# A count of the tiles that hold rows, and branches on TensorE that write zeros for steps past the count

## The chip, the cores and the metric

The kernel runs on one core of a Trainium2 chip. The time is that of one launch on the device, in microseconds (us). TensorE, the matrix engine, is called PE; VectorE is DVE, ScalarE is ACT, GpSimd is POOL, and SyncE, which issues most DMAs here, is SP. Each engine runs its own list of instructions in order, and waits on semaphores for the others.

## The reference

Two decoder layers over x, 16 sequences of 128 rows with 256 features, in float32. The first layer has causal attention with 16 heads, a recurrence over time in the place of cross attention, and a mixture of experts. The second has attention with 16 heads of 16 features, cross attention to a context with 16 heads of 128 features over 4 heads of keys and values, and a feed-forward part with ternary weights. The change concerns the mixture of experts, with 2048 rows, 16 experts, four experts for a row:

```
probs = softmax(h @ router_w.T)
top_vals, top_idx = top_k(probs, 4)
top_vals = top_vals / max(top_vals.sum(-1), 1e-09)
comb = zeros((N, E)).at[arange(N)[:, None], top_idx].add(top_vals)
g = einsum('nh,ehi->eni', h, w_gate)
u = einsum('nh,ehi->eni', h, w_up)
y = einsum('eni,eih->enh', silu(g) * u, w_down)
routed = einsum('enh,ne->nh', y, comb)
shared = silu(h @ sh_gate) * (h @ sh_up) @ sh_down
return routed + sigmoid(h @ sh_gate_w) * shared
```

## The kernel before

The kernel does not compute every expert for every row. While the shared expert runs, GpSimd scatters each normed row, four times, into a DRAM buffer `hs` that has a stretch of 2048 rows for each of the 16 experts. The rows of an expert stand together at the start of its stretch. Each stretch is cut into tiles of 128 rows. There are 8192 routed rows, so at least 64 tiles hold rows and at most 64+15 = 79 do; which ones, is known only at run time.

`tile_map` (L759 to L799) therefore builds a map on the chip. For every candidate tile DVE decides whether it holds rows (`per`, then `key`, which is 16 for a tile without rows and less for one with), ranks the candidates so that tiles with rows come first, and PE turns ranks into two lists of 128 numbers in `pmap`: the expert of the tile, and the row of `hs` where it starts. DVE copies them into `tmapT` (L798).

Then the pipeline at L1292 to L1296 works through the first NTILES = 79 entries of the map, whatever they hold, in NTILES + LAG = 85 steps. A step s works on several tiles at once, each in another stage:

- `fetch` (L746) for tile s, on SP: load the tile's start row from `tmapT` into a register, and start the DMA `hx <- hs`. The tile buffer has four slots.
- `turn_in` (L932) for tile s-2: two PE transposes into `pht`, and an ACT copy to `hxT`.
- `inner` (L941) for tile s-3: every eight tiles, PE loads eight expert numbers from `tmapT` (L943); gate and up products into `pgu` (L952); silu on ACT (L957), product with the up half on DVE (`eact`, L959).
- `turn_act` (L962) for tile s-5: two PE transposes into `pat`, a DVE copy to `eactT` (L968).
- `outer` (L971) for tile s-6: the down products into `pey` (L975), a copy `ey` on whichever of ACT and DVE the scheduler chooses (L981), and an SP store `hs <- ey`.

The four PSUM tiles `pht`, `pgu`, `pat` and `pey` come from one pool of four buffers, so that a stage takes over the buffer of the same stage a step before, or one like it, and waits for the copy or activation that read it.

After its stages each step calls `beside(s)` (L1226), which puts other work between the steps. It gathers finished rows back by GpSimd (`back_rows`, L1209: indirect DMAs out of `hs`), adds them to x on DVE (`back_sums`, L1218), and spreads the second layer's attention over the steps from 36 on: its scores `sc` (L1128) with maxima `nm` (L1131), `scT` (L1146) with exponents on ACT (L1150), values `zsT` (L1158), `zq` (L1169) with the division `z` on DVE (L1174), and the transposes `pqT` and `pkT` (L1105) of what DVE prepares in `spread` (L1110). At step 81 it issues the loads of the cross attention's weights Wk, Wq and Wv on SP (L1256); Wo follows after the last step (L1264). Cross attention begins with `pk` (L1315) and `proj` (L1349).

The order of PE's instructions in this part is the order in which the code is written (`tc.manual_schedule(engines={ET})`); the order on the other engines is chosen by a scheduler, from estimated times, within what the data allow. The loop is unrolled when the program is built, and before the change the program has no branch but the one with which every engine enters it.

```
for s in range(NTILES + LAG):
    for f, lag in ((fetch, 0), (turn_in, 2), (inner, 3), (turn_act, 5), (outer, LAG)):
        if 0 <= s - lag < NTILES and not (f is fetch and s in where):
            f(s - lag)
    beside(s)
```

Of the kernel before, what the change touches and what calls it, by code (L numbers as in the profile page):

```python
# [17 lines left out]
P = 128  # L18
B = 16
S = 128  # L20
D = 256
NK = D // P
# [8 lines left out]
TOPK = 4  # L31
IMOE = 176
# [4 lines left out]
NTILES = B * TOPK + E - 1  # L37
# [15 lines left out]
def decoder(ctx, tc, a, out):  # L53
    nc = tc.nc
    V, A, PE, GP = nc.vector, nc.scalar, nc.tensor, nc.gpsimd
# [701 lines left out]
    tmapT = rt.tile([1, 2, P], I32, name="tmapT")  # L757

    def tile_map():  # L759
# [169 lines left out]
    psum2.close()  # L929
    pools["wide"] = ctx.enter_context(tc.tile_pool(name="wide", bufs=4, space=PSUM, side="right", reuse_waits="tile"))  # L930

    def turn_in(j):  # L932
        hx = live[j]
        pt = tps.tile([P, NK, P], F32, tag="t", name="pht")
        for k in range(NK):
            PE.transpose(pt[:, k, :], hx[:, k * P : (k + 1) * P], ident)  # L936
        hT = mp.tile([P, NK, P], F32, tag="hxT", name="hxT")
        A.copy(hT, pt)  # L938
        live[j] = hT

    def inner(j):  # L941
        if j % NB == 0:
            _, vals = nc.values_load_multi_w_load_instructions(  # L943
                tmapT[0:1, 0, j : j + NB], engines=[ET], min_val=0, max_val=E - 1,
                skip_runtime_bounds_check_because=why,
            )
            for i, v in enumerate(vals):
                held[j + i] = v
        hT = live[j]
        pg = tps.tile([P, 2 * IMOE], F32, tag="t", name="pgu")  # L950
        for k in range(NK):
            PE.matmul(  # L952
                pg, hT[:, k, :], wgu[:, k, bass.ds(held[j], 1), :].rearrange("p e i -> p (e i)"),
                start=k == 0, stop=k == NK - 1,
            )
        s = mp.tile([P, IMOE], F32, tag="esilu", name="esilu", bufs=2)
        A.activation(s, pg[:, :IMOE], AF.Silu)  # L957
        act = mp.tile([P, IMOE], F32, tag="eact", name="eact")
        softmax.last = V.tensor_tensor(act, s, pg[:, IMOE:], ALU.mult).ins  # L959
        live[j] = act  # L960

    def turn_act(j):  # L962
        act = live[j]
        pt = tps.tile([P, NK, P], F32, tag="t", name="pat")
        for k in range(2):
            PE.transpose(pt[:HM, k, :], act[:, k * HM : (k + 1) * HM], ident)  # L966
        aT = mp.tile([HM, 2, P], F32, tag="eactT", name="eactT")
        V.tensor_copy(aT, pt[:HM])  # L968
        live[j] = aT

    def outer(j):  # L971
        aT = live.pop(j)
        py = tps.tile([P, D], F32, tag="t", name="pey")
        for k in range(2):
            ins = PE.matmul(  # L975
                py, aT[:, k, :], wd[:, bass.ds(held[j], 1), k, :].rearrange("p e d -> p (e d)"),
                start=k == 0, stop=k == 1,
            )
        last_pe[:] = [ins.ins]
        y = mp.tile([P, D], F32, tag="ey", name="ey")  # L980
        nc.any.tensor_copy(y, py)  # L981

        ins = nc.sync.dma_start(hs[bass.ds(where[j], P), :], y).ins
        for group in ("stores", "fetches", "gathers"):
            tc.declare_no_dep(ins, group=group, reason="each tile has rows of its own")
        tc.add_to_no_dep_group("stores", ins)

# [230 lines left out]


    LAG, FIRST, APART = 6, 36, 2
    GATHER = TOPK + E - 1 + LAG + 2
    LEAD = 6 * NKV

# [399 lines left out]
```

## Time and profile before

| what | value |
|---|---|
| median of 3 runs | 1679.83 us (1673.32 to 1681.09) |
| the profiled execution | 1683.29 us |
| its span, first to last instruction | 1681.6 us |
| mean granted clock of TensorE | 0.986 of full |
| first full product of an expert's tile on PE (step 3) | 762.25 us |
| a full step, from `pht` to the next `pht` | 2.50 us (1008.90 to 1011.39) |
| last `pey` (step 84) | 1032.42 us |
| first `proj` of cross attention | 1033.31 us |
| DMA `hx <- hs`, issue to landing | 2.1 us |
| DMA `hs <- ey`, issue to landing | 1.9 us |
| the ten loads of expert numbers on PE's sequencer | 0.588 to 0.779 us each |

The profile is of one execution; its times are counted from the start of the span. A line of a timeline gives start and duration in us, the engine, the line of the code, the operation, output and inputs by the names of the program, the partitions and elements, and how many instructions are put together in it; a bracket at the end is the time that the engine had stood idle and the work that released it. "PEld" are PE's weight loads, which run beside its matmuls. In the lines of the table of windows stand the stretch, its length, the busy time of PE, PEld, DVE, ACT and POOL with their counts, PE's granted clock, the share of the DMA engines and GB/s. The section on queues has, for each, packets, megabytes and the share of the 16 DMA engines' time.

### The profile page before, as it was taken

To read this page: it belongs to the slowest core of one execution; us is meant where nothing else is said; L and a number is where in the kernel's file an instruction comes from. 1 tells how busy PE (TensorE), PEld (TensorE's weight loads), DVE (VectorE), ACT (ScalarE), POOL (GpSimd) and SP (SyncE) were. 2 spreads that over 40 slices of the span, in tenths; PEclk is the share of its full clock that TensorE was granted. 3 is DMA by queue.
4 is the path that set the end of the run, shared out by engine and by line. 5 is a ranking of instruction groups with operands and counts; after the bars stand their busy time and mean duration, and the time that the engine had idled before them with its cause. 6 is when DMAs were issued, how large, how long until landed. Compare 5 with 4: busy or idle time off the path is not lost.

```text
span 1681.6 us, 27336 instructions
## 1 busy us (share of the span) xinstructions
PE 1630.0 (97%) x9824; PEld 1152.2 (69%) x9824; DVE 957.4 (57%) x2491; ACT 808.2 (48%) x2205; POOL 569.2 (34%) x586
## 2 busy tenths in 40 slices
PE   8999999999999999999899999999999999999996
PEld 4666666666665685656576777777777777787774
DVE  2333486457536667623345556567666666666756
ACT  3444454445444444113334545666666666665553
POOL 2010132244024234031246445654444444432420
PEclk9999999999999999999999999999999999999998
DMA  9990000000000019123353335000000000000000
GB/s 301 404 352 1 0 7 7 20 26 20 0 26 32 7 40 270 42 80 113 99 154 107 107 96 176 17 11 14 8 8 7 8 8 8 8 8 10 4 4 13
DMA packets 91662, 110.24 MB, mean 66 GB/s; under 512 B 8647, under 2 KB 66951, under 8 KB 91527
## 3 DMA queue, kind: packets, MB, share of 16 engines
q1 hardware_dynamic: 83094, 89.55, 16.5%
q0 software_dynamic: 6144, 16.79, 3.2%
q10 hardware_dynamic: 2288, 2.14, 0.4%
q8 instruction: 79, 1.29, 0.3%
q14 instruction: 57, 0.46, 0.1%
HBM read 54.06 MB, written 54.39 MB: 64 GB/s over the span
## 4 chain that ended last, share of the span: by engine, by line
PE 53%; DVE 2%; ACT 2%; issue 1%; POOL 1%; DMA 1%; SPq 0%; POOLq 0%; ACTq 0%; DVEq 0%
PE acc_x L1415 6%; PE proj L1349 6%; PE pgu L952 5%; PE pey L975 4%; PE sc L1380 3%; PE z L1400 3%; PE acc_sh L732 2%; PE pg L714 2%; PE pu L714 2%; PE pkv L1089 2%; PE pk L1315 2%; PE pT L1392 2%; PE pv L1315 1%; PE ss L1363 1%; PE sc L1128 1%
## 5 line engine op out<-in xcount | busy, mean ns | idle before, releaser
L189 ACT ACTIVATE sc<-sc,nmax 128x128 f32<-128x128 f32 x512 | 198.9, 389 | 169.9 <-DVE nmax L186 140.4
L186 DVE TENSOR_REDUCE nmax<-sc 128x4 f32<-128x512 f32 x128 | 87.3, 682 | 162.8 <-POOL sc L589 160.9
L589 POOL TENSOR_SCALAR_AFFINE_SELECT sc<-sc 128x512 f32<-128x512 f32 x64 | 42.9, 670 | 318.6 <-ACT sc L588 313.4
L1349 PEld LDWEIGHTS proj<-hc,wbig 128*128 128x128 f32 x1024 | 124.0, 192 | 29.2 <-issue 23.7
L125 POOL TENSOR_TENSOR rq<-rq,mhalf 128x4 f32<-128x4 f32 x64 | 67.8, 1059 | 209.7 <-DVE rq L1372 193.5
L595 PE MATMUL projv<-wv,hT 128*128 128x512 f32 x256 | 124.2, 608 | 3.3 <-ACT qT L578 3.3
L1415 PE MATMUL acc_x<-wbig,zT 128*128 128x256 f32 x512 | 124.8, 386 | 0.7 <-ACT zT L1406 0.7
L1349 PE MATMUL proj<-hc,wbig 128*128 128x128 f32 x1024 | 124.6, 275 | 0.1
L576 PE MATMUL proj<-hT,wq 128*128 128x512 f32 x256 | 122.6, 602 | 0.5 <-ACT hT L156 0.5
L576 PE MATMUL proj<-hT,wk 128*128 128x512 f32 x256 | 120.9, 595 | 1.1 <-ACT sc L588 1.0
L174 PEld LDWEIGHTS acc_l<-wo,zT 128*128 128x128 f32 x512 | 96.4, 190 | 36.6 <-issue 26.6
L174 PE MATMUL acc_l<-wo,zT 128*128 128x256 f32 x512 | 121.3, 380 | 0.0
L952 PE MATMUL pgu<-wbig,hxT 128*128 x316 | 111.8, 478 | 2.1 <-PE pht L936 0.8
L1415 PEld LDWEIGHTS acc_x<-wbig,zT 128*128 128x128 f32 x512 | 93.3, 190 | 23.6 <-issue 11.3
L125 POOL TENSOR_TENSOR ss<-ss,mhalf 128x32 f32<-128x32 f32 x16 | 87.5, 5471 | 45.7 <-DVE ss L1098 45.6
L189 ACT ACTIVATION_READ_ACCUMULATOR sc<-sc,nmax 128x1 f32 x512 | 95.5, 187 | 0.0
L1383 DVE SCALAR_TENSOR_TENSOR sc<-sc,rq,mask 128x128 f32<-128x128 f32 x256 | 77.5, 343 | 29.0 <-PE sc L1380 24.0
L1209 POOL DMA_INDIRECT back<-hs,idx x64 | 64.1, 1002 | 84.4 <-DMA hs<-ey 68.0
L576 PEld LDWEIGHTS proj<-hT,wk 128*128 128x128 f32 x256 | 48.7, 191 | 64.1 <-issue 52.6
L968 DVE COPY eactT<-pat 88x256 f32<-88x256 f32 x79 | 33.0, 418 | 98.2 <-PE pat L966 98.2
L624 PEld LDWEIGHTS z<-probT,v 128*128 128x128 f32 x512 | 68.1, 194 | 30.2 <-issue 29.9
L975 PE MATMUL pey<-wd,eactT 88*128 x316 | 84.7, 391 | 0.9 <-ACT hxT L938 0.9
(344 smaller groups left out, 3508.3 us busy)
## 6 DMA issues: line engine op xcount, KB each, us to landing
hs<-zero SPq DMA_DIRECT2D x16, 2048.0 KB, 19.0
hx<-hs SPq DMA_DIRECT2D x79, 128.0 KB, 2.1
hs<-ey SPq DMA_DIRECT2D x79, 128.0 KB, 1.9
wbig<-in_L_ffn_w_gate_dram SPq DMA_DIRECT2D x2, 1408.0 KB, 13.6
wbig<-in_L_ffn_w_up_dram SPq DMA_DIRECT2D x2, 1408.0 KB, 17.1
wd<-in_L_ffn_w_down_dram SPq DMA_DIRECT2D x2, 1408.0 KB
wq<-in_L_attn_W_Q_dram SPq DMA_DIRECT2D x8, 256.0 KB, 4.0
vT<-in_ctxT_dram ACTq DMA_DIRECT2D x8, 256.0 KB, 2.5
```

Of the source, the lines that this page charges most:

```text
L125: power.last = GP.tensor_tensor(v, v, mhalf[:, :n], ALU.pow).ins
L174: ins = PE.matmul(acc[:, t, :], zT[:, i, :], w[:, h0 + i, :], start=False, stop=last and i == 3, skip_group_check=True,)
L186: softmax.last = V.tensor_reduce(nmax, sc, AX.X, ALU.max, negate=True).ins
L189: A.activation(p[:, i, :], sc[:, i, :], AF.Exp, bias=nmax[:, i : i + 1], accum_out=rs[:, i : i + 1])
L576: PE.matmul(pj, w[:, k, h, :], hTs[g][:, k, :], start=k == 0, stop=k == NK - 1)
L595: PE.matmul(pv, hTs[g][:, k, at], wv[:, k, 4 * hq : 4 * hq + 4, :].rearrange("p h e -> p (h e)"), start=k == 0, stop=k == NK - 1,)
L624: PE.matmul(pz[:, i, :], v[:, i, :], pT[:, i, :], start=True, stop=True)
L952: PE.matmul(pg, hT[:, k, :], wgu[:, k, bass.ds(held[j], 1), :].rearrange("p e i -> p (e i)"), start=k == 0, stop=k == NK - 1,)
L975: ins = PE.matmul(py, aT[:, k, :], wd[:, bass.ds(held[j], 1), k, :].rearrange("p e d -> p (e d)"), start=k == 0, stop=k == 1,)
L1349: PE.matmul(pj[:, i, :], wqx[:, n, k, i * DH : (i + 1) * DH], hTs[b][:, k, :], start=k == 0, stop=k == NK - 1,)
L1383: V.scalar_tensor_tensor(sc[:, i, :], psc[:, i, :], rq[:, i : i + 1], mask, ALU.mult, ALU.add)
L1415: PE.matmul(accs[b][:, :D], zT[:, i, :], wox[:, 4 * n + i, :], start=n == 0 and i == 0, stop=n == NKV - 1 and i == 3,)
```

## The change

The map also counts the tiles with rows: DVE compares each `key` with 15.5, two PE products with a column of ones sum the result into a free column of `pmap`, and DVE copies the sum into `nusedT`. The four stages no longer issue their work when called. Each returns three things: a function that issues its products on PE, the PSUM tile they write, and a function that issues the rest (copy, silu, product on DVE, store). A step first issues all its products, then all rests. The expert numbers are loaded ahead of the step's products (`numbers`).

From step SURE = 64+6 = 70 on the products stand in a branch on PE, with the count in a register that is loaded at step 70: if the count is above s-6, the number of the oldest tile in the step, the products are done; otherwise, when none of the step's tiles holds rows, PE writes zeros into the same PSUM tiles, with one matmul of a single row for each. The rests and `beside(s)` are done in either case.

```diff
+        used = rt.tile([P, 2], F32, name="used")
+        V.tensor_scalar(used, key, float(B) - 0.5, None, ALU.is_lt)
...
+            for h in range(2):
+                PE.matmul(
+                    pmap[0:1, 2 * P : 2 * P + 1], ones[:, 0:1], used[:, h : h + 1], start=h == 0, stop=h == 1,
+                )
+        V.tensor_copy(nusedT, pmap[0:1, 2 * P : 2 * P + 1])
         V.tensor_copy(tmapT, pmap[0:1, : 2 * P].rearrange("p (j n) -> p j n", j=2))
...
     def turn_in(j):
         hx = live[j]
         pt = tps.tile([P, NK, P], F32, tag="t", name="pht")
-        for k in range(NK):
-            PE.transpose(pt[:, k, :], hx[:, k * P : (k + 1) * P], ident)
-        hT = mp.tile([P, NK, P], F32, tag="hxT", name="hxT")
-        A.copy(hT, pt)
-        live[j] = hT
+
+        def products():
+            for k in range(NK):
+                PE.transpose(pt[:, k, :], hx[:, k * P : (k + 1) * P], ident)
+
+        def rest():
+            hT = mp.tile([P, NK, P], F32, tag="hxT", name="hxT")
+            A.copy(hT, pt)
+            live[j] = hT
+
+        return products, pt.rearrange("p k n -> p (k n)"), rest
...
     LAG, FIRST, APART = 6, 36, 2
+    SURE = B * TOPK + LAG
...
             for s in range(NTILES + LAG):
-                for f, lag in ((fetch, 0), (turn_in, 2), (inner, 3), (turn_act, 5), (outer, LAG)):
-                    if 0 <= s - lag < NTILES and not (f is fetch and s in where):
-                        f(s - lag)
+                if s < NTILES and s not in where:
+                    fetch(s)
+                if 0 <= s - 3 < NTILES:
+                    numbers(s - 3)
+                if s == SURE:
+                    nused = nc.values_load(
+                        nusedT[0:1, 0:1], engines=[ET], min_val=SURE - LAG, max_val=NTILES,
+                        skip_runtime_bounds_check_because=why,
+                    )
+                stages = [
+                    f(s - lag) for f, lag in ((turn_in, 2), (inner, 3), (turn_act, 5), (outer, LAG))
+                    if 0 <= s - lag < NTILES
+                ]
+
+                with tc.If(nused > s - LAG) if s >= SURE else ExitStack() as some:
+                    for products, _, _ in stages:
+                        products()
+                if s >= SURE:
+                    with some.Else():
+                        for _, t, _ in stages:
+                            PE.matmul(t, zeros_b[:, : t.shape[0]], zeros_b[:, : t.shape[1]], start=True, stop=True)
+                for _, _, rest in stages:
+                    rest()
                 beside(s)
             load_last_weights()
```

`inner`, `turn_act` and `outer` are split in the same way. `outer` no longer records its last product in `last_pe`.

In the built program the branch is laid out in line: at each of the 15 steps PE has a compare with a branch, the block of products with a jump over the block of zeros, and the block of zeros with a jump to what follows. Each of the other four engines has a jump at the same place of its list, although it has nothing in either block. Where the scheduler cut a list, instructions no longer change places across the jump: from step 70 on SP issues each fetch after the store of the step before, where it had two fetches and then two stores.

More of the change, by code (lines that the diff above doesn't have):

```diff
@@ L757, in decoder @@
     tmapT = rt.tile([1, 2, P], I32, name="tmapT")
+    nusedT = rt.tile([1, 1], I32, name="nusedT")
     def tile_map():
@@ L934, in turn_in, with numbers @@
         pt = tps.tile([P, NK, P], F32, tag="t", name="pht")
-        for k in range(NK):
-            PE.transpose(pt[:, k, :], hx[:, k * P : (k + 1) * P], ident)
-        hT = mp.tile([P, NK, P], F32, tag="hxT", name="hxT")
-        A.copy(hT, pt)
-        live[j] = hT
-    def inner(j):
+        def products():
[6 more added lines that the diff above has]
+        return products, pt.rearrange("p k n -> p (k n)"), rest
+    def numbers(j):
         if j % NB == 0:
@@ L948, in inner, with products, rest @@
                 held[j + i] = v
+    def inner(j):
         hT = live[j]
         pg = tps.tile([P, 2 * IMOE], F32, tag="t", name="pgu")
[L951 to L960, printed above, removed]
+        def products():
+            for k in range(NK):
+                PE.matmul(
+                    pg, hT[:, k, :], wgu[:, k, bass.ds(held[j], 1), :].rearrange("p e i -> p (e i)"),
+                    start=k == 0, stop=k == NK - 1,
+                )
+        def rest():
+            s = mp.tile([P, IMOE], F32, tag="esilu", name="esilu", bufs=2)
+            A.activation(s, pg[:, :IMOE], AF.Silu)
+            act = mp.tile([P, IMOE], F32, tag="eact", name="eact")
+            softmax.last = V.tensor_tensor(act, s, pg[:, IMOE:], ALU.mult).ins
+            live[j] = act
+        return products, pg, rest
     def turn_act(j):
@@ L964, in turn_act, with products, rest @@
         pt = tps.tile([P, NK, P], F32, tag="t", name="pat")
[L965 to L969, printed above, removed]
+        def products():
+            for k in range(2):
+                PE.transpose(pt[:HM, k, :], act[:, k * HM : (k + 1) * HM], ident)
+        def rest():
+            aT = mp.tile([HM, 2, P], F32, tag="eactT", name="eactT")
+            V.tensor_copy(aT, pt[:HM])
+            live[j] = aT
+        return products, pt[:HM].rearrange("p k n -> p (k n)"), rest
     def outer(j):
@@ L973, in outer, with products, rest @@
         py = tps.tile([P, D], F32, tag="t", name="pey")
[L974 to L986, printed above, removed]
+        def products():
+            for k in range(2):
+                ins = PE.matmul(
+                    py, aT[:, k, :], wd[:, bass.ds(held[j], 1), k, :].rearrange("p e d -> p (e d)"),
+                    start=k == 0, stop=k == 1,
+                )
+        def rest():
+            y = mp.tile([P, D], F32, tag="ey", name="ey")
+            nc.any.tensor_copy(y, py)
+            ins = nc.sync.dma_start(hs[bass.ds(where[j], P), :], y).ins
+            for group in ("stores", "fetches", "gathers"):
+                tc.declare_no_dep(ins, group=group, reason="each tile has rows of its own")
+            tc.add_to_no_dep_group("stores", ins)
+        return products, py, rest
     U = B * NKV
@@ L1292, in decoder @@
             for s in range(NTILES + LAG):
[L1293 to L1295 removed]
+                if s < NTILES and s not in where:
[6 more added lines that the diff above has]
+                        skip_runtime_bounds_check_because=why,
+                    )
+                stages = [
[11 more added lines that the diff above has]
+                    rest()
                 beside(s)
```

## The prediction

> **What bounds the kernel now.** I read the page's busy times first, then the timeline of TensorE (PE) around the steps the change touches, then all engines there, then the table of windows.
>
> ```profile
> PE 1630.0 (97%) x9824; PEld 1152.2 (69%) x9824; DVE 957.4 (57%) x2491; ACT 808.2 (48%) x2205; POOL 569.2 (34%) x586
> ...
> q8 instruction: 79, 1.29, 0.3%
> ```
>
> PE is busy 97% of the span, so PE work taken out pays in full wherever nothing else is late. The second line is used below. Whether something else is late is read where the work is taken out. PE in the last steps of the pipeline (start, duration, line, tile):
>
> ```profile
> 1015.08 0.44 PE L936 MATMUL pht<-ident,hx 128*128 128x128 f32 x2
> 1015.35 1.35 PE L952 MATMUL pgu<-wbig,hxT 128*128 x4
> 1016.54 0.38 PE L966 MATMUL pat<-ident,eact 128*88 128x128 f32 x2
> 1016.76 1.03 PE L975 MATMUL pey<-wd,eactT 88*128 x4
> 1017.62 0.38 PE L936 MATMUL pht<-ident,hx 128*128 128x128 f32 x2
> ...
> 1020.04 1.13 PE L975 MATMUL pey<-wd,eactT 88*128 x4 [0.22 <-ACT hxT L938]
> 1021.10 1.08 PE L1158 MATMUL zsT<-probT,vaug 128*32 128x128 f32 x32
> ...
> 1028.49 1.15 PE L1128 MATMUL sc<-kT,qT 16*128 16x128 f32 x26 [0.33 <-DVE z L1174]
> ...
> 1033.31 3.74 PE L1349 MATMUL proj<-hc,wbig 128*128 128x128 f32 x32
> ```
>
> The first four lines are step 79, 1015.08 to 1017.62. A bracket says how long PE stood idle and for whom: here PE already waits a little, for ACT at 1020.04 and for DVE at 1028.49. The other engines in the same stretch:
>
> ```profile
> 1015.76 2.07 ACT L1150 ACTIVATE probT<-scT 128x512 f32<-128x512 f32 x4
> ...
> 1017.69 0.40 ACT L938 COPY hxT<-pht 128x256 f32<-128x256 f32 x1
> ...
> 1018.11 1.28 ACT L957 ACT_TABLE_LOAD   x1
> ...
> 1019.41 0.32 ACT L957 ACTIVATE esilu<-pgu 128x176 f32<-128x176 f32 x1
> ...
> 1020.76 0.68 DVE L1110 TENSOR_TENSOR spread<-qk,ss 128x512 f32<-128x512 f32 x1
> ...
> 1028.02 0.42 DVE L1174 TENSOR_TENSOR z<-zq,rs 128x256 f32<-128x256 f32 x1
> ...
> 1029.48 2.48 DVE L1131 TENSOR_REDUCE nm<-sc 128x4 f32<-128x512 f32 x4 [1.04 <-PE sc L1128]
> ```
>
> To see: ACT is in four exponents, a copy, a table load and a silu from 1015.76 to 1019.73 without a gap, and DVE's spread, z and maxima (nm) sit between PE's pieces. These two chains end only 0.3 to 1 us before PE wants them.
>
> **The change part by part.**
>
> How many steps skip. The reference's router on these inputs gives 73 tiles with rows (the sum over experts of rows/128, rounded up; one expert is a row over a tile's edge, so 72 is possible). Step s branches on nused > s-6, so steps 70 to 78 do their products and 79 to 84 write zeros.
>
> PE work removed. A full step is 2.50 us apart in the timeline (1008.90 to 1011.39): pht 0.22, pgu 1.19, pat 0.22, pey 0.87, from start to next start. Steps 79 to 84 hold 2 pht, 3 pgu, 5 pat and 6 pey: 0.44+3.57+1.10+5.22 = 10.33 us. Zeros added: 16 one-row matmuls of bf16. Row L165 has the same form with 512 columns, two in 0.60 us where one takes 0.374, so 0.22 each; at 256 to 352 columns I take 0.12, in all 1.9 us. If PE set the pace everywhere, the gain would be 8.4 us.
>
> What of it reaches the end. Copies, silu, products on DVE, stores and gathers all stay, and a zero matmul waits for its PSUM tile just as the product did (four buffers, four stages a step). So I walk the stretch with PE short.
> - Step 79's zeros are done near 1015.7. Step 80's pey needs the tile that silu and eact of step 79 read. ACT reaches that silu at 1019.41 whatever PE does, since the exponents wait for scT, which is unchanged. Eact follows near 1020.1, so zsT starts near 1020.4 (before 1021.10): of 4.5 us saved 0.7 arrive.
> - pqT waits for spread, 0.68 on DVE behind eact: near 1021.75 (before 1022.11). Gain here 0.4.
> - Steps 81 and 82 write five zeros in place of 3.4 us of products: zq near 1023.7 (before 1026.40), 2.7 ahead.
> - sc's fourth tile needs DVE's z, which stands behind back_sums' adds (1.51 for two at 1026.07, another 0.43), and these behind gathers that wait for stores. I place z's end between 1025.8 and 1026.6 (before 1028.44): 1.9 to 2.6 ahead.
> - Then 2.48 of maxima on DVE, eactT, pey of steps 83 and 84, and proj. The first proj also needs Wq from DMA: issued 1024.28, landed 5.8 later, near 1030.1, now queued on SP behind a store. proj starts 1031.0 to 1031.75 against 1033.31.
>
> So 1.5 to 2.4 us arrive, taken as 2.0; the rest of the 8.4 becomes PE waiting for ACT, DVE and DMA.
>
> The count. One DVE compare and one 1x1 copy (about 0.15 each) before the map's copy, hidden because the first fetch needs the map long before PE reaches step 2 at 761.35, and two tiny fp32 matmuls (4 records; the pmap row L794 has its records 0.11 apart) inside a stage where PE is at 1.00: +0.3 us.
>
> Products ahead of rests. Up to step 69 PE's order is unchanged; one hxT copy stands behind a weight activation of 0.55 on ACT, but is wanted a step (2.5 us) later: 0. From 70 on each SP fetch comes behind the store of the step before: it lands 2.1 us after issue (page, hx), wanted 1.1 later: 0, and up to 1 us a step if that cover is gone. The numbers' load (0.6 us, L943) moves ahead of pht, under the sequencer's lead (1.6 us in steady steps): +0.1.
>
> The branches, which no row of before shows as such. PE gets a compare at each of 15 steps and one jump in a true step, two when false; ACT, DVE, POOL and SP get a jump a step, and what is queued behind theirs are the copies, silus, adds and stores above, for which PE waits. Lower bound 0: PE's sequencer runs 1.6 us ahead in full steps. Nearest row: all engines jump once at the start, between a barrier at 0.69 to 0.74 and first instructions at 0.80 to 0.90, so at most 0.17 each. In steps 70 to 78 it hides (no engine but PE is near full there): +0.1. In 79 to 84 some four jumps lie in the ACT, DVE and PE chain: +0.6. [...]
>
> The clock. [...] At 787.47 PE had been idle 2.42 us, and the clock fell for the next matmuls (last but third figure: PEclk):
>
> ```profile
> 785.00:790.00 5.00, 2.58 (x12) 1.88 (x12) 1.00 (x3) 2.71 (x8) 1.09 (x3) 0.90 0.38 79
> 790.00:795.00 5.00, 5.00 (x20) 3.52 (x19) 1.07 (x4) 1.28 (x4) 0.00 (x0) 0.76 0.67 243
> ```
>
> The step begun at 788.59 ended at 792.77, 4.18 in place of 2.50: one such drop costs 1.7 us. [...] By the row the waits of 1.5 to 2.5 us that my walk leaves near 1022 and 1025 can each bring another: 0 to 3.4, part of it under waits for other engines. I take 0.9, half a drop.
>
> Sum: -2.0 +0.3 +0.1 +0.1 +0.6 +0.9 = 0.0 us. The profiled execution took 1683.3 us (span 1681.6), and its like after would take 1683.3; the median of the three runs of before is 1679.8, and I forecast 1679.8. The runs of before spread over 7.8 us, so 0.5%, or 8.4 us, is about what a measurement of this kernel can tell from no change.
>
> **The rivals.**
>
> A. The skipped work lands whole: -8.4+0.3 = -8.1, 1671.7. For it: PE at 97%. Against it: the ACT chain to 1019.73 and the brackets above, which leave PE no room to move up. Chance 0.07.
>
> B. Slower: a jump throws away what the sequencer had fetched, and each is paid by a new fetch. Price: the page's q8 line has 79 packets in 0.3% of 16 engines over the span, 1.0 us each; with a DMA's way from issue to landing (2.1 for hx), some 2 us a jump. Place: steps 70 to 84 on PE, 9+12 jumps. The sequencer's lead is then gone at each step, so 1 to 2 us are bare in a true step (9 to 18 us) and 12 to 24 in the false ones, of which the skipped work pays up to 8: +13 to +34, taken as +20, 1700. It decides from 0.56 us bare a step (8.4/15). For it: fetches are sequential in the trace, one packet behind the other. Against it: the jump at the start at 0.17 or less. Chance 0.28 that over 8.4 us are lost, this or jumps of 0.6 to 1.2 each.
>
> C. The change doesn't do what it says: the count reads 79, or steps go true, and nothing is skipped. Then +0.5 for count and order, +0 to 2.4 for branches: near 1681. The count itself, 73 of 79, argues against it. Chance 0.04.
>
> **How the numbers follow.** About unchanged, by my walk, 0.61; A 0.07 (its -8.1 lies at the bound; with the runs' spread I put 0.05 beyond it); B 0.28; C 0.04, within 0.5%. So faster by over 0.5% 0.05, within 0.67, slower 0.28. The range goes from 1673, short of A, to 1700, B's value: 0.07 is left out below and 0.13 above.
>
> **What would show it.** TensorE from 1015 to 1033: 16 short zero matmuls in place of pht to pey; zsT near 1020.4, behind silu and eact of step 79; proj's first near 1031.4; PE idle there up by 6 us, named ACT and DVE; the clock in windows after 1017. Steps 70 to 78 still 2.50 us apart; if each is 3 us or more with idle put down to issue, B is right. proj at 1025 would be A; full pgu after 1017, C. I am wrong if the slow place lies before step 70, where I cost the new order at nothing.

## The result and the profile after

The changed kernel takes 1679.08 us, median of 20 runs (1676.15 to 1686.52); the kernel before takes 1675.15 (1671.52 to 1682.36) in as many, of which the three that the prediction had to go by lay high. The ratio is 1.0028, with an interval of 1.0018 to 1.0039: slower by some 4.7 us, within the 0.5% that the prediction set as the bound of no change, but with the sign certain. The forecast of 1679.8 us stood for no change against the median of three runs, and that median came down by 4.7 us with 20.

The two profiled executions do not show the loss at first sight: the span after is 1679.9 us against 1681.6. The table of windows tells why. The first two rows are of before, the next two of the changed kernel (stretch, its length, busy time of the five engines, PE's granted clock, DMA share, GB/s):

```profile
780.00:800.00 20.00, 17.13 (x73) 12.06 (x74) 4.45 (x16) 7.59 (x22) 4.56 (x8) 0.91 0.39 121
800.00:850.00 50.00, 44.18 (x185) 30.97 (x185) 15.23 (x45) 18.61 (x53) 13.56 (x21) 0.90 0.35 107
```

```profile
780.00:800.00 20.00, 17.84 (x85) 12.75 (x86) 4.87 (x16) 8.23 (x24) 4.55 (x8) 1.00 0.43 135
800.00:850.00 50.00, 44.40 (x209) 31.45 (x208) 19.10 (x55) 20.10 (x59) 16.93 (x25) 1.00 0.39 121
```

The execution of before that was profiled happened to lose clock here (0.91 and 0.90, against 1.00 in the changed kernel's), long before the change acts; it had 1683.3 us, 8 above its kernel's median. The work there is the same in both kernels. From pey of step 6 to pey of step 49 it took 133.6 us (768.18 to 901.81), the changed kernel's 126.4 (767.74 to 894.09). So spans can't be set against each other; stretches of the timeline can, from one event to another. I use three, in us:

- A, from pey of step 69 to the first scT of step 78: the steps that branch and do their products.
- B, from that scT to the first proj: the steps that skip.
- C, from that proj to the first pkT of cross attention: what follows.

| | A | B | C |
|---|---|---|---|
| before | 34.7 | 19.3 | 6.2 |
| changed, this profile | 38.6 | 20.5 | 6.1 |

The change loses 3.9 us in A, where it was to cost next to nothing, and 1.2 in B, where the walk was to gain 2 before the clock and the jumps. B in the changed kernel, on PE (start, duration, line, tile; in the bracket the idle time before it and what ended it):

```profile
1010.48 1.17 PE L1182 MATMUL scT<-q2T,kT 32*128 32x128 f32 x32
1011.47 0.27 PE L1350 MATMUL pht<-zeros_b 1*128 1x256 bf16 x1
1011.58 0.31 PE L1350 MATMUL pgu<-zeros_b 1*128 1x352 bf16 x1
...
1014.65 0.36 PE L1350 MATMUL pat<-zeros_b 1*88 1x256 bf16 x1 [1.04 <-ACT hxT L952]
1016.65 0.39 PE L1350 MATMUL pey<-zeros_b 1*128 1x256 bf16 x1 [1.64 <-DVE eact L982]
1016.97 1.93 PE L1194 MATMUL zsT<-probT,vaug 128*32 128x128 f32 x32
1018.83 1.12 PE L1141 MATMUL pqT<-ident,spread 128*128 128x128 f32 x4
...
1026.38 3.78 PE L1372 MATMUL pk<-wbig,hc 128*128 128x512 f32 x4 [0.37 <-DVE nm L1167]
...
1030.98 3.84 PE L1406 MATMUL proj<-hc,wbig 128*128 128x128 f32 x32 [0.51 <-ACT ey L1015]
```

To see: the zeros cost what they were taken for (0.11 from one to the next), PE waits for ACT and DVE as foreseen, and then zsT takes 1.93 in place of 1.08, pqT 1.12 in place of 0.66, pk 3.78 where the same four products take 1.88 later on. That is half speed. The windows of the same stretch say it in the clock (last but third figure):

```profile
1010.20:1013.60 3.40, 2.47 (x40) 1.57 (x39) 3.01 (x12) 2.99 (x5) 3.40 (x2) 1.00 0.12 41
...
1013.00:1016.00 3.00, 0.93 (x3) 0.26 (x3) 0.25 (x1) 2.97 (x6) 2.13 (x5) 0.60 0.13 44
1016.00:1019.00 3.00, 2.35 (x34) 1.65 (x35) 1.91 (x6) 1.11 (x5) 2.39 (x3) 0.50 0.29 87
...
1025.00:1028.00 3.00, 2.63 (x18) 1.54 (x15) 2.37 (x4) 0.37 (x1) 0.00 (x0) 0.50 0.96 323
```

In A two things are to be seen. On DVE, at step 75, the division z stands behind adds and copies, where in the profile of before it followed the reciprocal directly. The first two rows are of before, the others of the changed kernel:

```profile
997.60 0.26 DVE L1172 RECIPROCAL rs<-zq 128x16 f32<-128x16 f32 x1
997.89 0.42 DVE L1174 TENSOR_TENSOR z<-zq,rs 128x256 f32<-128x256 f32 x1
```

```profile
990.62 0.26 DVE L1208 RECIPROCAL rs<-zq 128x16 f32<-128x16 f32 x1 [1.97 <-PE zq L1205]
990.79 0.39 DVE L1254 SCALAR_TENSOR_TENSOR x<-back,wts,x 128x256 f32<-128x256 f32 x1
991.10 0.33 DVE L982 TENSOR_TENSOR eact<-esilu,pgu 128x176 f32<-128x176 f32 x1
991.35 0.48 DVE L1254 SCALAR_TENSOR_TENSOR x<-back,wts,x 128x256 f32<-128x256 f32 x1
991.75 0.41 DVE L997 COPY eactT<-pat 88x256 f32<-88x256 f32 x1
992.08 0.41 DVE L1210 TENSOR_TENSOR z<-zq,rs 128x256 f32<-128x256 f32 x1
```

PE's sc then waits 0.80 us for z, and the pgu that follows, at 994.51, takes 2.37 in place of 1.35: the clock again, at half for 3.41 us from 993.15, which is worth 1.7 us of full work. And on ACT, in seven of the nine steps from 70 to 78, hxT is released by the wrong product (in the other two ACT was busy until then):

```profile
1006.61 0.37 ACT L952 COPY hxT<-pht 128x256 f32<-128x256 f32 x1 [1.17 <-PE pat L993]
1006.88 0.32 ACT L980 ACTIVATE esilu<-pgu 128x176 f32<-128x176 f32 x1
1007.59 0.37 ACT L1015 COPY ey<-pey 128x256 f32<-128x256 f32 x1 [0.38 <-PE pey L1008]
```

pht began at 1004.90 and was done by 1005.3, but hxT, which copies it, starts at 1006.61, with pat. In the trace PE's semaphore is not raised between the end of pht and the end of pgu at 1006.47, and hxT starts with the raise of the first pat; in the profile of before it was raised at the end of pht. The built program gives the reason: both sides of this step's branch raise the semaphore by 8 in all, the side of the products by 4 at the end of pgu and by 1 with each product of pat and pey, and pht's products do not raise it by themselves. The pgu of the next step then waits up to 0.24 us for ey. No wait of PE in A is for a load of hx, so the order of fetches behind stores on SP cost nothing that shows.

### The profile page after: what moved, and what is told of

Its sections match the earlier page's. It is cut to its first block, busy times and chain, and to the rows that moved or that the text cites. A ratio compares the mean times of both kernels' runs of the same rounds, so it can differ in the third digit from the quotient of the medians.

```text
span 1679.9 us, 27293 instructions
## 1 busy us (share of the span) xinstructions
PE 1623.6 (97%) x9794; PEld 1146.7 (68%) x9794; DVE 956.9 (57%) x2493; ACT 806.9 (48%) x2205; POOL 568.2 (34%) x586
## 4 chain that ended last, share of the span: by engine, by line
PE 53%; DVE 3%; ACT 2%; issue 1%; POOL 1%; DMA 0%; POOLq 0%; SPq 0%; ACTq 0%; DVEq 0%
PE proj L1406 7%; PE acc_x L1472 6%; PE pgu L973 5%; PE sc L1437 3%; PE pey L1008 3%; PE z L1457 3%; PE acc_sh L732 2%; PE pk L1372 2%; PE pg L714 2%; PE pu L714 2%; PE pkv L1125 2%; PE pT L1449 2%; PE pv L1372 1%; PE ss L1420 1%; PE sc L1164 1%
## 5 line engine op out<-in xcount | busy, mean ns | idle before, releaser
L973 PE MATMUL pgu<-wbig,hxT 128*128 x304 | 105.7, 471 | 1.2 <-ACT ey L1015 0.5
L1443 POOL TENSOR_TENSOR sc<-sc,rsum 128x512 f32<-128x512 f32 x64 | 66.8, 1044 | 38.4 <-DVE rsum L1442 18.9
```

The lines of the kernel that those rows point to most:

```text
L973: PE.matmul(pg, hT[:, k, :], wgu[:, k, bass.ds(held[j], 1), :].rearrange("p e i -> p (e i)"), start=k == 0, stop=k == NK - 1,)
```

## The experiments

The theory from this profile: the loss has two parts, and neither is the jump itself. In A, a branch cuts the lists of the other engines (DVE's order at step 75) and makes signals late; in B, PE runs out of work, its clock is halved (0.50 in the windows above), and what it has left takes twice as long (pk 3.78 in place of 1.88). One rival is that the jumps cost time on the engines. Another is that the new order of products and rests does. The first four kernels ran together.

**Zeros without a branch (e_static).** In place of the branch:

```diff
-                with tc.If(nused > s - LAG) if s >= SURE else ExitStack() as some:
-                    for products, _, _ in stages:
-                        products()
-                if s >= SURE:
-                    with some.Else():
-                        for _, t, _ in stages:
-                            PE.matmul(t, zeros_b[:, : t.shape[0]], zeros_b[:, : t.shape[1]], start=True, stop=True)
+                for products, t, _ in stages:
+                    if s < 79:
+                        products()
+                    else:
+                        PE.matmul(t, zeros_b[:, : t.shape[0]], zeros_b[:, : t.shape[1]], start=True, stop=True)
```

> No branch: steps 79 to 84 write zeros always, decided when the program is built (right for these inputs, which have 73 tiles with rows); the count stays, the rests stay. Clock theory (PE short of work loses its clock in the steps that skip): the stretch from scT of step 78 to the first proj, 19.3 us before and 20.5 in the changed kernel, stays at 20 to 20.6, with PEclk near 0.7 and pk x4 near 3.8 us; total +0.5 to +1.5 us against before. Jump and queue theory (branches, and the lists they cut on DVE and SP, cost the time): the stretch shrinks to 17 or 18 us and the total is 1.5 to 2.4 us below before.

**Only the new order (e_order).** The branch is replaced by `for products, _, _ in stages: products()`.

> No branch and no zeros: all products done, but all products of a step ahead of all its rests, the numbers loaded earlier, and the count in the map. Clock theory and queue theory: as before in every stretch, within 0.5 us, total +0.3 us. If the new order of products and rests is what costs: steps 70 to 78 lose 0.8 us or more here too, and the steps before 70 lose as well.

**All branches true (e_true).** `tc.If(nused > s - LAG - 20)`. The edit does more than turn the branches one way. The count's lower bound of 64 makes the condition always true, and it was settled when the program was built: the trace has no compare or jump on PE and no load of the count, where that of the changed kernel has 24 compares and jumps:

```profile
L1344 PEldq COMPARE_BRANCH  x24: 65/179/312, 969.6 to 1026.4; - x24
```

(Shortest, median and longest in ns, then the first and last start.) So e_true has the blocks, the cut lists and the late signals of the changed kernel, but PE takes no branch.

> All branches stay, their condition is loosened by 20 tiles so that all 15 take the true side and do their products. Clock theory: the stretch from scT of step 78 to proj is back at 19.3 us with PEclk 1.00, total below the changed kernel by about 1 us. Queue theory: the wait of sc for DVE z at step 75 (0.80 us) and the clock drop behind it stay, so steps 70 to 78 still lose about 3.5 us against before, total +3 to +4. Jump theory: every one of the 15 steps is longer by 0.2 us or more with PE idle put down to issue, total +3 or more with the loss spread evenly.

**Six branches (e_six).** `SURE = 73 + LAG`.

> The branches begin at step 79, six in all, so that every branch taken is the zero side; steps 70 to 78 have none. Clock theory: the stretch from scT to proj stays at 20 to 20.6 us, total +1 to +1.5 us against before. Queue theory: sc's wait for z at step 75 is gone, steps 70 to 78 are as before, and of the +4 us of the changed kernel about 3 are gone. Jump theory: the stretch keeps its loss and the steps 70 to 78 win back 0.8 us only.

Measured, with the later kernels in one table (ratio to before on the same chip; A, B, C from the one profile of each):

| kernel | branches on PE | A | B | C | ratio (95% interval) |
|---|---|---|---|---|---|
| e_order | 0 | 34.7 | 20.2 | 6.1 | 0.9996 (0.9983 to 1.0009) |
| e_static | 0 | 34.7 | 19.4 | 6.4 | 0.9981 (0.9968 to 0.9995) |
| e_six | 6 | 34.7 | 21.1 | 6.1 | 1.0001 (0.9986 to 1.0015) |
| e_true | 0, lists cut at 15 | 38.6 | 20.1 | 6.1 | 1.0006 (0.9993 to 1.0019) |
| a_again (changed) | 15 | 40.0 | 20.9 | 8.2 | 1.0028 (1.0016 to 1.0041) |
| e_twice | 30 | 40.0 | 20.4 | 6.7 | 1.0032 (1.0016 to 1.0047) |
| e_four | 52 | 37.2 | 19.4 | 7.1 | 1.0000 (0.9989 to 1.0012) |
| e_fix | 15 | 41.4 | 21.3 | 6.1 | 1.0035 (1.0019 to 1.0051) |
| e_fix2 | 15 | 36.0 | 21.6 | 8.0 | 1.0018 (1.0003 to 1.0033) |
| e_late | 0 | 35.3 | 19.3 | 6.2 | 1.0006 (0.9996 to 1.0016) |
| e_warm | 0 | 37.3 | 22.5 | 6.6 | 1.0008 (0.9992 to 1.0024) |
| e_warm2 | 0 | 34.7 | 19.9 | 6.1 | 0.9997 (0.9984 to 1.0009) |
| e_warm3 | 0 | 34.7 | 16.2 | 6.6 | 0.9981 (0.9969 to 0.9993) |
| e_warm4 | 0 | 34.7 | 16.6 | 6.1 | 0.9970 (0.9954 to 0.9987) |
| e_drop | 0 | 31.0 | 20.9 | 6.1 | 0.9973 (0.9959 to 0.9987) |
| e_best | 52 | 37.2 | 21.2 | 7.5 | 1.0022 (1.0006 to 1.0037) |

From the first four: A is 34.7 where no list is cut in it. It is 38.6 where the lists are cut, and e_true, in which PE takes no branch, agrees with the changed kernel to 0.01 us (38.62 and 38.63) and has the same waits, 0.80 for z and 0.24 for ey. So A's loss belongs to the cut lists and late signals, and PE's compares and jumps add nothing to it. The totals agree only in part: e_six, with A back at 34.7, has a ratio whose interval lies below that of the changed kernel, but e_true's total is only 1.6 us above e_order's by medians (1676.67 and 1675.07), less than its A says; the clock drop that A holds in this one profile need not come in every execution.

The new order of products and rests costs nothing in A or in the total, but 0.9 us in B. Besides sc's wait for z, 0.50 in place of 0.33, proj waits for ACT's ey in e_order, as it does for the same 0.51 in the changed kernel, where in the profile of before ey began 0.25 after proj:

```profile
1027.06 3.84 PE L1401 MATMUL proj<-hc,wbig 128*128 128x128 f32 x32 [0.51 <-ACT ey L1015]
```

B is 18.9 to 19.4 in e_static although PE's work is gone, as the clock theory had it, and 20.5 to 21.1 with branches and zeros. But the total of e_static is 3 us below before, where the clock theory gave +0.5 to +1.5, and its profile has A+B+C at 60.5 against 60.2. It was run again twice (e_static2 and e_static3, for comparison on other chips): 0.9982 (0.9968 to 0.9996) and 0.9981 (0.9967 to 0.9995), with A 34.7, B 18.9 and 19.4, C 6.6 and 6.7. So by these profiles those 3 us are not in the stretches that the change touches. They lie ahead of them: set against e_order on the same chip, e_static's pey of step 6 comes 2.8 us earlier and its way from there to pey of step 69 is 2.3 shorter, 5.1 of the 5.8 by which its span is shorter, and both kernels have the same instructions there. What differs is where the clock fell (first two rows e_order, then e_static):

```profile
665.00:680.00 15.00, 13.27 (x39) 7.08 (x38) 12.24 (x18) 6.21 (x8) 3.02 (x3) 0.89 0.48 97
880.00:900.00 20.00, 17.93 (x109) 13.07 (x108) 11.01 (x34) 6.67 (x20) 14.73 (x12) 0.91 0.39 125
```

```profile
665.00:680.00 15.00, 13.26 (x44) 7.18 (x41) 13.13 (x19) 5.12 (x7) 1.92 (x2) 1.00 0.42 80
880.00:900.00 20.00, 18.56 (x118) 13.65 (x117) 12.32 (x34) 7.32 (x21) 11.55 (x9) 1.00 0.40 128
```

Why e_static's executions should be spared such drops is not shown. Its total is therefore no evidence that the skipped work pays.

> e_static a second time, for comparison on the same chip: zeros in steps 79 to 84 without a branch. All theories: 2 to 4 us below before, the stretch from scT to proj near 19.4 us at a PEclk near 0.5.

> e_static on the same chip as e_warm4, to see whether the clock held in the profile also shows in the total. All theories: 2 to 4 us below before (ratio 0.9975 to 0.999).

**The order on DVE mended (e_fix).** One constraint in the changed kernel, for which each add of `back_sums` is kept in `back_sums.last`:

```diff
-        V.reciprocal(rs, heads_[:, :, HD1])
+        with tc.issue_after(back_sums.last) if back_sums.last else ExitStack():
+            V.reciprocal(rs, heads_[:, :, HD1])
...
```

> The changed kernel with its 15 branches, and one constraint for DVE's list: the reciprocal behind zq is issued after the adds of the rows gathered back, which gives at step 75 the order that before had (adds, eactT, reciprocal, z). Cut-list theory (the jumps cut DVE's list and the scheduler's new order inside a block makes sc wait for z, which then costs clock): from pey of step 69 to scT of step 78 it takes 35.5 to 36 us in place of 38.6 (34.7 before), total 2 to 2.8 us below the changed kernel. Jump theory: the stretch keeps 37.5 us or more.

**Twice the jumps (e_twice).** The loop over `stages` in both sides is cut in two halves, each with a branch of its own.

> Each step's branch is split in two that follow each other (turn_in and inner, then turn_act and outer), so that every engine takes twice the jumps, with no work of other engines between the two. Jump theory (a jump itself costs each engine time): total 2 to 4 us above the changed kernel, the added time spread over all steps from 70. Cut-list theory: jumps as such cost nothing that shows; total within 1 us of the changed kernel, or 2 to 2.8 us below it, since here DVE's list at step 75 has the adds ahead of the reciprocal again.

**One-row zeros as filling (e_warm).** In e_static, `for _ in range(8 if s == 79 else 1)` around the zero matmul.

> As e_static (no branch, zeros from step 79 on), but step 79 writes each of its four zero tiles eight times, so that PE is kept at work for about 3.5 us of the time in which it waited for ACT. Clock theory: PEclk stays at 1.00 in more of the stretch, zsT still starts 5.4 us after scT since ACT sets it, but pqT to pk are no longer at half speed, and the stretch from scT to proj falls from 19.4 to 15.5 to 17 us; total 2 to 4 us below e_static although PE does more. If the clock is not what costs there: the stretch is 19.4 us or longer, total the same or up to 1 us above.

**The tiles without rows dropped (e_drop).** In e_order `NTILES` becomes 73 in the three conditions of the loop over steps.

> No branch, no zeros, and no work at all for tiles 73 to 78 on any engine (no fetch, copy, silu, product on DVE, or store; right for these inputs, which have 73 tiles with rows). Clock theory: PE still has to wait for ACT's exponents in step 79 and loses its clock; the stretch from scT to proj is 16 to 19 us, total 0 to 3 us below e_static. If what limits the stretch is the work that the rests leave on ACT, DVE and SP: the stretch falls to 13 to 15 us, and the total is 4 to 6 us below e_static.

These four ran on another chip, where before takes 1696.6 us and the spans are longer ahead of the change too. e_fix gave no verdict: sc no longer waits for z, but pht of step 74 waits 2.62 us there, as pht of that step does for 2.33 in e_warm, which has no branch; in e_fix PE runs at half speed behind it (pgu 2.55, pey 1.91, zq 1.06), in e_warm at full (1.35, 1.03, 0.60). e_twice has the ratio of the changed kernel with twice the branches, but its A is of another make: as its expectation had it, sc does not wait for z there, and pht has that wait, 2.71 us, with a clock drop at it (the pgu behind it takes 2.48 in place of 1.35). Against e_warm its A is 2.7 longer, of which 1.7 are lost clock, 0.4 the longer wait and 0.24 a wait for ey, so that little is left for the jumps. e_drop gains 0.27%, 3.8 us by medians: A is 31.0 in place of the 34.7 of before, but with the tiles' work gone from all engines PE waits in B 5.75 us for DVE's spread, that is for the attention's own chain, and B is 20.9 in place of 19.3. e_warm went against its expectation and taught something else:

```profile
1025.94 1.03 PE L1349 MATMUL pht<-zeros_b 1*128 1x256 bf16 x8
1026.82 1.35 PE L1349 MATMUL pgu<-zeros_b 1*128 1x352 bf16 x8
1028.01 1.70 PE L1349 MATMUL pat<-zeros_b 1*88 1x256 bf16 x8
```

```profile
1026.00:1028.00 2.00, 2.00 (x22) 1.45 (x16) 0.00 (x0) 1.99 (x4) 2.00 (x1) 1.00 0.98 332
1028.00:1030.00 2.00, 2.00 (x13) 1.68 (x11) 0.25 (x1) 1.98 (x4) 2.00 (x4) 0.55 1.04 378
```

PE is busy 2.00 us of 2.00 with one-row matmuls, and the clock falls all the same, 2 us after they begin (eight of pat take 1.70 where eight of pht took 1.03). So e_warm was no test of the clock, and the next filling was of full height.

**The changed kernel again, a branch for each stage, and full-height filling.** a_again is the changed kernel. e_four moves the `with tc.If` inside the loop over stages. e_warm2 puts 32 transposes ahead of step 79's zeros and 6 ahead of step 80's into pht's tile.

> The changed kernel as it is, for comparison on the same chip with the three that follow. All theories: 2 to 6 us above before; from pey of step 69 to scT of step 78 38 to 39 us, with hxT released by pat in place of pht in steps 70 to 78.

> One branch for each stage in place of one for each step, 54 in all in place of 15, so that each product's signal to ACT and DVE stands in a block of its own. Signal theory (inside one branch the signal of pht is only given with a later product of the block, so that hxT, silu and all behind them start about 1.4 us late): hxT is released by pht again, the true steps are 2.50 us apart and pgu no longer waits for ey; from pey of step 69 to scT 35 to 36 us, total 1 to 3 us below the changed kernel although there are over three times as many jumps. Jump theory: 39 more jumps on each engine, total 3 to 8 us above the changed kernel.

> As e_static, but ahead of the zeros of step 79 PE does 32 transposes of 128x128, and 6 ahead of those of step 80, into the PSUM tile that the zeros then fill: 4.2 us of full-height work in the time in which PE waits for ACT. (The eightfold one-row zeros did not keep the clock.) Clock theory: PEclk stays 1.00 through the stretch, zsT comes 5.4 us after scT as before, and scT to proj falls from 19.4 to 15 to 16.5 us; total 2.5 to 4 us below e_static2. If the clock is not the price: scT to proj is 19 us or more, total the same or above.

a_again repeats the loss (A 40.0), and here half the clock lasts into proj, whose first 32 take 5.97 in place of 3.74. e_four has 52 branches by its built program (its expectation counted 54) and the time of before, where the jump theory had 3 to 8 us more than the changed kernel: that theory falls. Its ACT shows the signal in its place:

```profile
983.22 0.37 ACT L952 COPY hxT<-pht 128x256 f32<-128x256 f32 x1 [0.99 <-PE pht L948]
```

But A is 37.2, not 35 to 36. DVE's list is cut anew, and its order makes PE wait at other places (0.39 for ey, 0.60 for eactT, 0.67 for spread, 0.24 for ey), which are 1.9 of the 2.5 us that A is longer than in before. So e_four changes two things, and the next kernels take them apart. e_warm2 kept PE at full speed up to zq (zsT 1.08, pqT and zq 0.66 each), but its transposes held up hxT on ACT, zsT came 2.2 us later, and nothing was won.

**The order alone again, the late signal alone, and filling that holds nobody up.** e_fix2 is e_fix. e_late is e_order with the products in steps 70 to 78 issued as pgu, pat, pht, pey. e_warm3 is e_static with

```diff
...
+                        for _ in range({(80, 1): 16, (80, 2): 6}.get((s, i), 0)):
+                            PE.transpose(t[:, :P], ident[:, : t.shape[0]], ident)
                         PE.matmul(t, zeros_b[:, : t.shape[0]], zeros_b[:, : t.shape[1]], start=True, stop=True)
```

> e_fix a second time (all branches, the reciprocal behind zq issued after the adds), since its first profile had a wait of 2.62 us of pht at step 74 that a kernel without branches on the same chip had too. If DVE's order at step 75 is the larger part of the loss in the true steps: from pey of step 69 to scT of step 78 35.6 to 36 us (38.6 to 40.0 in the changed kernel, 34.7 before), the rest of the loss being the 0.2 to 0.5 us a pair of steps that late signals cost; total 2 to 3 us below the changed kernel (ratio to before 1.0005 to 1.0015). If the late signals are the larger part: the stretch stays above 37 us and the ratio at 1.002 to 1.004.

> No branch, all products done, but in steps 70 to 78 PE does pht behind pgu and pat, so that hxT on ACT starts as late as it does behind the signals of a branch, with all lists of the other engines uncut. If late signals alone cost: the stretch from pey of step 69 to scT of step 78 grows from 34.7 to 36 us or more and the total is 1 to 3 us above before. If they only cost together with the cut lists: 34.7 to 35.3 us, total within 1 us of before.

> As e_static, but step 80 does 16 transposes of 128x128 into pgu's tile and 6 into pat's ahead of their zeros, in the very gaps in which PE waits for ACT, and nothing ahead of step 79's zeros; the 38 transposes of e_warm2 kept the clock to zq but held ACT's hxT up, so that zsT came 2.2 us later. Clock theory: zsT again 5.4 to 6 us after scT, PEclk 1.00 to zq, and scT to proj 15.5 to 18 us in place of 18.9 to 19.4; total 1 to 3 us below e_static (ratio to before 0.9965 to 0.998). If PE's clock is not what sets the stretch: 18.9 us or more, and the ratio at 0.998 or above.

e_fix2: A falls from 38.6 and 40.0 to 36.0, and sc runs through. The order on DVE, with the clock that its wait costs, is the larger part of A's loss, 2.6 to 4.0 us; 1.3 remain. e_late: A is 35.3, so a late hxT without cuts costs 0.6, less than the 1.3 that its first theory asked. It is a copy of the case and not the case: PE waits there for hxT (0.32) and eactT (0.29 and 0.31), in the changed kernel for ey. What of the 1.3 lies with the late hxT, the late silu and ey, or the cuts on ACT was not separated. e_fix2's ratio is below the changed kernel's but the intervals overlap, and its B and C (29.6 together) have PE at half speed from zsT at 1010.89 (1.94 in place of 1.08) into proj (5.82 in place of 3.74).

e_warm3 answers for B. PE in its gaps, and the clock there:

```profile
1004.20 1.97 PE L1349 MATMUL pgu<-ident 128*128 128x128 f32 x16
1006.10 0.32 PE L1350 MATMUL pgu<-zeros_b 1*128 1x352 bf16 x1
1006.35 0.85 PE L1349 MATMUL pat<-ident 128*88 128x128 f32 x6
...
1008.14 1.08 PE L1194 MATMUL zsT<-probT,vaug 128*32 128x128 f32 x32
```

```profile
1004.00:1008.00 4.00, 3.42 (x26) 2.55 (x25) 0.67 (x3) 3.97 (x9) 4.00 (x3) 1.00 1.00 333
1008.00:1012.00 4.00, 3.22 (x47) 2.23 (x47) 2.32 (x8) 2.62 (x8) 1.69 (x3) 1.00 1.04 394
1012.00:1015.00 3.00, 2.75 (x41) 2.08 (x41) 2.84 (x8) 0.72 (x3) 2.09 (x4) 1.00 1.09 379
```

PE does 2.8 us more work than in e_static, zsT comes 0.9 later, and proj comes 3.1 earlier (16.2 in place of 19.4). The clock falls once more, to 0.67 in the window from 1015 to 1018, under pk and the first proj. That the half clock is what ate the skipped work is shown for this stretch. The total doesn't show it: e_warm3's ratio, 0.9981, is e_static's. For the total it was tried once more, both kernels on one chip, with a branching kernel that has both remedies (e_best: e_four with the transposes in the zero sides of step 80).

> e_warm3 on the same chip as e_static3. Clock theory: 1.5 to 3 us below e_static3, stretch from scT to proj 16 to 17 us. If the clock that the profile shows is won back later, or is lost elsewhere in other executions: within 1 us of e_static3.

> The branch at run time kept, with one branch a stage as in e_four, and in the zero sides of step 80 the 16 transposes into pgu's tile and 6 into pat's of e_warm3. Signal and clock theories together: the stretch from scT to proj, 19.4 us in e_four, falls to 16.3 to 17.5 us; the true steps stay at 37.2 us from pey of step 69 to scT (34.7 before); total 1.5 to 3 us below before (ratio 0.998 to 0.999). If the clock in that stretch does not set the total: ratio 0.9995 to 1.0005, as e_four.

e_warm4 is 1.0 us below e_static3 by medians (1671.02 and 1672.01), with intervals that overlap, though B repeats at 16.6 and the mean clock of its 12 executions is 0.989 to 0.992 against 0.986 to 0.989: the clock is the better one in its executions too, but in the total the gain is at most partly there, and it stays open why. e_best missed. After a wait of 0.83 for eactT PE fell to half speed within the first 1 us of the transposes, sixteen of them took 3.31 us in place of 1.97, zsT came 9.2 us after scT, and its ratio is above e_four's, on another chip and with intervals that just overlap. Of kernels that decide at run time none beat before.

## Why the prediction was wrong

What held. 73 tiles, 16 zeros in steps 79 to 84, 0.11 to 0.15 us each; PE waiting for ACT's silu and DVE's eact at pey of step 80, with zsT 0.64 us nearer to scT than before where 0.7 was worked out. (In e_static pey waits for eactT only, and zsT is 1.8 nearer; 1.1 us of B's loss against e_static arises there.) The walk itself gave proj 17.0 to 17.8 us after scT, and near full clock it comes after 16.2 and 16.6 (e_warm3 and e_warm4, without branches). That jumps as such cost next to nothing held: PE's compares and jumps take 65 to 312 ns each on its sequencer, A is the same without them (e_true), and 52 branches left the total where it was (e_four). Rival B, the refetch, is refuted: the instruction queue q8, from which it took its price, moved as many packets as before,

```profile
q8 instruction: 79, 1.29, 0.3%
```

and none of the 24 compares and jumps on PE, 312 ns at most, lasts as long as one of its packets, which the price has at 1.0 us. Rival A fell for the reason given, and the clock besides. Rival C fell, since the zeros were written in steps 79 to 84.

What failed is two terms of the sum.

The first is the branches in steps 70 to 78: "it hides (no engine but PE is near full there): +0.1". Measured: +3.9 in one profile and +5.3 in the other. A branch was costed as time of the sequencers and as order on SP. What it does to the lists it cuts was not followed. DVE's order inside the blocks was there to read in the built program, as was the count for which hxT waits; the prediction named the copies, silus and adds that are queued behind a jump, but asked only how long the jump holds them. 2.6 to 4.0 us are DVE's order at step 75 with the clock drop behind it (e_fix2), and 1.3 the late signals and other cuts, not separated. The term "Products ahead of rests" was too small as well: it put nothing on B, where the new order alone costs 0.9 us (e_order).

The second is the clock: "I take 0.9, half a drop." The clock fell, but no run shows half a drop: in the changed kernel's B the half clock cost 4.1 us, from start to next start against before: 0.85 in zsT, 0.87 in pqT and pkT, 0.4 in sc, 1.99 in pk; in a_again 2.2 more in proj. The error was to price one drop by its model in the row of 787 us, where PE had full work behind the gap and was back at 1.00 after 3.41 us. Here the work behind the gap is itself broken by waits, and the clock was at half for 6.83 us from 1013.62 and for 6.83 again from 1023.87. Nor does that row describe how the drop came: a single wait of 2.42 was not needed. Ahead of 1013.62 PE was busy 2.47 of 3.40 us (the row from 1010.20), its only long wait was the one of 0.93, and the waits of 1.04 and 1.64 came when the clock was down already. From the end of scT, near 1011.65, PE had done nothing but one-row zeros.

One reading was loose without harm: z does not end before PE wants it, since the bracket at 1028.49 is PE's wait for it.

The walk and the clock together account for B: 2.7 to 3.1 us gained near full clock (e_warm3, e_warm4) and 4.1 lost to the clock come to a loss of 1.0 to 1.4, and 1.2 was measured. A, B and C together are 5.0 us longer than in before's profile and 9.0 in a_again, around the 4.7 that the runs give. How much of each falls into a given execution changes with the clock.

That 1679.08 lies close to the 1679.8 of the forecast is chance: the median that it started from was 4.7 us above what 20 runs gave.

## What to carry to other kernels

Here a branch on one engine was paid in the lists of the others (A 38.6 in place of 34.7, also in e_true, where PE takes no branch): before costing a branch's jumps, compare the order of each engine's list on both sides of the cut and the counts for which the consumers of the branch's products wait; a branch for each producer kept the signals apart (hxT released by pht again in e_four), and many small ones were cheaper here than one (e_four, ratio 1.0000 against 1.0028). Work taken from the engine that is the bound was worth only what the next chain left, 2.7 to 3.1 us of the 8.4 that the prediction counted, and less than that with the clock at 0.50 under what remained, which took 4.1 us back. Where a skip is wanted, these runs favour a count known when the program is built, which fits only inputs with that count, and the tile left out of every engine's work (e_drop, ratio 0.9973); leaving out its products alone (e_static) did not shorten the stretches that it touches. And an experiment on a branch is to be checked in its trace: a condition that the bounds decide leaves no branch to measure (e_true).

## What the runs showed of the hardware

One-row matmuls back to back did not hold TensorE's clock in e_warm: it went from 1.00 to 0.55 with PE busy 2.00 of 2.00 us. With 16 transposes of full height in 1.97 us it stayed at 1.00 in e_warm3, while in e_best, behind a wait of 0.83, the same sixteen took 3.31. In the traces of before and of the changed kernel the clock is either full or half, and it is at half for 3.41 or 6.83 us at a time, but for the last stretch, which the end of the trace cuts off at 10.61 and 19.78: 3.41 from 788.95 in before, 6.83 twice in the changed kernel's B. In a_again the clock was not regained in 19 us of work that was broken by short waits (0.50 from 1018 to 1037).
